# Attention's sums, maxima and quotients turned by VectorE's 32x32 block transposes in place of TensorE's transposes and the side PSUM bank

## The chip, the core and the metric

The kernel runs on one core of a Trainium2 chip. The metric is the device time of the launch in microseconds (us). One core has TensorE (PE, matrix products, with its weight loads PEld), VectorE (DVE), ScalarE (ACT), GpSimd (POOL) and SyncE (SP, which here only issues DMAs).

## What is computed

A transformer block over `x` of shape (4, 1024, 256): normalised attention with 16 heads of 16 dimensions, then a gated feed-forward network with ternary weights, each with a layer norm behind it and a residual.

```python
def _stable_softmax(x):
    x_max = jax.lax.stop_gradient(jnp.max(x, axis=-1, keepdims=True))
    exp_x = jnp.exp(jnp.clip(x - x_max, -50.0, 50.0))
    return exp_x / (jnp.sum(exp_x, axis=-1, keepdims=True) + EPS)
...
scores = jnp.einsum('bhqd,bhkd->bhqk', q, k) * scale
attn = _stable_softmax(scores)
out = jnp.einsum('bhqk,bhkd->bhqd', attn, v)
out = jnp.transpose(out, (0, 2, 1, 3)).reshape(B, S, D)
return out @ Wout.T
...
x = x + _layernorm(_L0_attn_ref(_layernorm(x, axis=-1), L0_attn_Wqkv, L0_attn_Wout), axis=-1)
x = x + _layernorm(_L0_ffn_ref(_layernorm(x, axis=-1), ...), axis=-1)
```

The kernel takes plain exponentials (no maximum is subtracted), so the reference's EPS has to be scaled by the largest exponential of a query: the quotient is `sum(e v) / (sum(e) + EPS * max(e))`. That is where sums, maxima and quotients come from.

## The kernel before

**Tiles and units.** Attention is cut into 32 units: batch `b` (4), group `g` of four heads (4), half `h` of the queries (2 of 512). In a unit every head has a slot of 32 partitions. A unit has 16 tiles; a tile is 128 keys by 512 queries for two heads. `exponentials(k)` (lines 521-529) makes a tile: two score matmuls `s` (L528) into one of three two-bank PSUM buffers (`ps`, tag `big`), and one ACT exponential `e` (L529) into a ring of eight. `weigh(k)` (L531-536) multiplies two tiles with the values: it accumulates into `acc`, one PSUM bank (`ps_acc`, one buffer), whose partition 32i+d is dimension d of head i, partition 32i+16 is the head's sum of exponentials, and whose 512 columns are queries. `rise(k)` (L538-545) keeps the running maximum over keys in `top` on DVE, for the first 128 queries of the half alone (the other queries need no EPS).

**The order.** A loop written out by hand (L1332-1363) makes three tiles, weighs what is ready, makes further tiles and then calls `side.take` once: a slot. `take` (L700-715) runs steps of the side chains that are due: at most one step with TensorE work in a slot (`Step(..., tensor=True)`), and steps without it as long as the slot's `room`, an estimate of DVE work, lasts. A step has a gap in slots, a flag for heavy ones (projections `p`, `pv`, `py`) and a `work` figure. The steps are: the next batch's layer norm and projections (`prologue`), the end of each unit (`divide`), the end of each half (`ending`), checks of the exponents' range (`bound`, `flag`), the loads of the stacks and the weights' rounding. All steps with a PSUM result share one bank, `misc` (L259-260).

**The end of a unit.** `unit_end` (L763-806) copies `acc` to SBUF as `o` (L328, DVE), which frees `acc`. `divide` (L558-584) sends `top` to DRAM and back as `folded`, which puts head and 32 keys on the partitions (L563, L566, SP queue); `fold` takes two maxima (L570); `run` puts four 128x128 TensorE transposes of `o` into the `misc` bank (L575) and a fifth of `folded` into unused columns of the same bank (`HOLE`, L577-578). Now queries are on the partitions: DVE reduces the maxima (`em`, L580), and `quotients` (L547-556) forms the denominators, inverts them and multiplies, into `on[h]` (128 queries x 4 x 256). The last group of the last batch uses `divide_last` (L586-600), which transposes `top` itself (L593) with no DRAM.

**The end of a half.** When its four groups are done, `ending` transposes `on` back in two steps of four TensorE transposes (L613) through `misc`, copies each to `oT` (L614; DVE, or ACT for the very last half), projects with the output weights `wo_sb` in two heavy steps `py` (L618-626), and then normalises and adds. For the last batch's second half these steps run among the first matmuls `pg` of the feed-forward network (`gated`, L924-940, one `side.take` after each pair of `pg` products, L1238-1241).

**The feed-forward network** (L924-1151) follows: matmuls `pg`, `ph` (L1015), `pz`, with two-term splits of the operands.

The lines that the change touches: the output weights' loads (L229-232), `on` (L249), `quotients`, `divide`, `divide_last`, `ending.transposes` (L606-616), the step list (L656) and `unit_end` (L766).

Of the kernel before, what the change touches and what calls it, by code (L numbers as in the profile page):

```python
# [10 lines left out]
F32 = mybir.dt.float32  # L11
# [4 lines left out]
ALU = mybir.AluOpType  # L16
AX = mybir.AxisListType
PSUM = bass.MemoryType.PSUM

P = 128  # L20
HEADS = 16
DH = 16
SLOT = 32
HPG = P // SLOT
# [1 line left out]
PARTS = 4  # L26
ROWS = PARTS * DH
RING = 8
HOLE = 20
TURN = 3  # L30
LN_EPS = 1e-5
SM_EPS = 1e-6
# [6 lines left out]
NQ = 512  # L39
WIDE = 1024  # L40
TPQ = NQ // P
# [89 lines left out]
def tile_fast(ctx: ExitStack, tc: tile.TileContext, x, wqk, wv, wo, w1, w1s, w2, w2s, h1, h1s, h2, h2s, w3, w3s, out, bad):  # L131
    nc = tc.nc
    B, S, D = x.shape
    HID = w1.shape[1]
    DC = D // P
    HC = HID // P
    NT = S // P
    NH = S // NQ
    HPT = P // DH
    GPT = HPT // HPG  # L140
# [3 lines left out]
    small = ctx.enter_context(tc.tile_pool(name="small", bufs=3))  # L144
# [52 lines left out]
    with ExitStack() as actx, ExitStack() as rctx:  # L197
# [21 lines left out]
        def load_rest():  # L219


            def load(out, in_):
                return lambda: nc.sync.dma_start(out=out, in_=in_)

            def load_half(b, h):
                return lambda: load_x(b, [h])

            rest = [load_half(2, h) for h in range(NH)]
            for c in range(DC):  # L229
                for h in range(HPT):  # L230
                    r = SLOT * (HPT * c + h)
                    rest.append(load(wo_sb[DH * h : DH * (h + 1), c, :], wo[r : r + DH, :]))
            rest += [load_half(b, h) for b in range(3, B) for h in range(NH)]
            rest += [load(scales[name], w) for name, w in (("w1", w1s), ("w2", w2s), ("h1", h1s), ("h2", h2s))]
            return rest + [load(w3s_sb, w3s.partition_broadcast(P))]
# [10 lines left out]
            nc.gpsimd.memset(t[:, :, :, DH : DH + 1], 1.0)  # L246
            vaug.append(t)

        on = [aw.tile([P, TPQ, D], F32, name=f"on{h}") for h in range(NH)]  # L249

        heads_bf = aw.tile([P, SLOT], BF16, name="heads_bf")
        nc.vector.memset(heads_bf, 0.0)
# [6 lines left out]
        def misc(name):  # L259
            return ps_misc.tile([P, NQ], F32, tag="misc", name=name)  # L260
# [66 lines left out]
        def to_vector(o, i, scale=1.0):  # L327
            nc.vector.tensor_scalar(o, i, scale, None, ALU.mult)  # L328
# [215 lines left out]
                top = tops[b, g, h]  # L544
                nc.vector.tensor_max(top, top if c > 1 else pair(k - 2)[:, :, :, 0:P], pair(k)[:, :, :, 0:P])  # L545

        def quotients(g, h, em, po):  # L547

            den = small.tile([P, TPQ, HPG], F32, tag="den", name="den")
            nc.vector.scalar_tensor_tensor(den[:, 0], em, SM_EPS, po[:, 0, :, DH], ALU.mult, ALU.add)  # L550
            nc.vector.tensor_copy(den[:, 1:], po[:, 1:, :, DH])
            nc.vector.reciprocal(den, den)
            nc.vector.tensor_mul(
                on[h][:, :, HPG * DH * g : HPG * DH * (g + 1)].rearrange("p t (i e) -> p t i e", e=DH),
                po[:, :, :, 0:DH], den.unsqueeze(3).to_broadcast([P, TPQ, HPG, DH]),
            )

        def divide(g, h, o, top):  # L558


            there = shuffle.tile([HPG, P, P], F32, tag="top", name="top_d")
            folded = work.tile([P, P // SLOT, P], F32, tag="folded", name="folded", bufs=1)
            nc.sync.dma_start(out=there.rearrange("i k q -> k i q"), in_=top.rearrange("p u n q -> p (u n) q"))  # L563

            def back():
                nc.sync.dma_start(out=folded, in_=there.rearrange("i (k s) q -> (i k) s q", s=P // SLOT))  # L566

            def fold():
                for n in (2, 1):
                    nc.vector.tensor_max(folded[:, 0:n], folded[:, 0:n], folded[:, n : 2 * n])  # L570

            def run():
                p = misc("po")
                for t in range(TPQ):
                    nc.tensor.transpose(p[:, t * P : (t + 1) * P], o[:, t * P : (t + 1) * P], ident)  # L575

                pm = p.rearrange("p (n s) -> p n s", s=SLOT)[:, :, HOLE : HOLE + P // (TPQ * HPG)]  # L577
                nc.tensor.matmul(pm, folded[:, 0], ident.rearrange("p (n k) -> p n k", n=TPQ * HPG), start=True, stop=True, is_transpose=True)
                em = small.tile([P, HPG], F32, tag="em", name="em")
                nc.vector.tensor_reduce(em, pm.rearrange("p (i n) k -> p i n k", i=HPG), AX.XY, ALU.max)  # L580
                po = p.rearrange("p (t i s) -> p t i s", t=TPQ, s=SLOT)
                quotients(g, h, em, po)

            return [Step(back, 2, False), Step(fold, 2, False, work=1), Step(run, 1, work=2)]

        def divide_last(g, h, o, top):  # L586


            def run():
                both = ps.tile([P, 2, NQ], F32, tag="big", name="po")  # L590
                po, pm = both[:, 0], both[:, 1].rearrange("p (i k) -> p i k", k=P)
                for i in range(HPG):
                    nc.tensor.transpose(pm[:, i], top[:, i // 2, i % 2], ident)  # L593
                for t in range(TPQ):
                    nc.tensor.transpose(po[:, t * P : (t + 1) * P], o[:, t * P : (t + 1) * P], ident)
                em = small.tile([P, HPG], F32, tag="em", name="em")
                nc.vector.tensor_reduce(em, pm, AX.X, ALU.max)
                quotients(g, h, em, po.rearrange("p (t i s) -> p t i s", t=TPQ, s=SLOT))

            return [Step(run, 1)]  # L600

        def ending(b, h, copy):

            st = {}

            def transposes(c):  # L606
                def run():
                    if c == 0:
                        st["oT"] = work.tile([P, DC, NQ], F32, tag="oT", name=f"oT_{b}_{h}", bufs=1)
                        st["y"] = (both if h else work).tile([P, TPQ, D], F32, tag="y", name=f"y_{b}_{h}", bufs=1)  # L610
                    pt = misc(f"po_{b}_{h}_{c}")
                    for t in range(TPQ):
                        nc.tensor.transpose(pt[:, t * P : (t + 1) * P], on[h][:, t, c * P : (c + 1) * P], ident)  # L613
                    copy(st["oT"][:, c, :], pt)  # L614

                return run

            def project(t0):  # L618
                def run():
                    py = misc(f"py_{b}_{h}_{t0}").rearrange("p (t d) -> p t d", d=D)  # L620
                    for i in range(2):
                        for c in range(DC):
                            by_slots(py[:, i, :], st["oT"][:, c, (t0 + i) * P : (t0 + i + 1) * P], wo_sb[:, c, :], start=c == 0, stop=c == DC - 1)
                    (copy if b == B - 1 else to_scalar)(st["y"][:, t0 : t0 + 2, :], py)

                return run

            def gather(i):
                def run():
                    st["mv"] = norms.gather([st["y"][:, j, :] for j in range(i, i + 2)], i, st.get("mv"))  # L630

                return run

            def root():
                st["ln"] = norms.root(st["mv"])

            def apply(i0):
                def run():
                    if b == B - 1 and i0 == 0:
                        st["to"] = norms.shift(st["ln"])  # L640
                    for i in range(i0, i0 + 2):
                        if b == B - 1:
                            norms.scale(st["y"][:, i, :], st["y"][:, i, :], st["to"], i)
                        else:
                            norms.apply(st["y"][:, i, :], st["y"][:, i, :], st["ln"], i)

                return run

            def residual(i):
                def run():  # L650
                    xr = xs[b][:, h * TPQ + i : h * TPQ + i + 2, :]
                    nc.vector.tensor_add(xr, xr, st["y"][:, i : i + 2, :])

                return run

            steps = [Step(transposes(c), 1, work=1) for c in range(DC)] + [Step(project(t), 2, heavy=True) for t in range(0, TPQ, 2)]  # L656
            tail = (
                [Step(gather(i), 1, False, work=1.6) for i in range(0, TPQ, 2)] + [Step(root, 0, False, work=0.3)]
                + [Step(apply(i), 1, False, work=1.2) for i in range(0, TPQ, 2)] + [Step(residual(i), 1, False, work=1) for i in range(0, TPQ, 2)]
            )  # L660
            if b < B - 1:

                return steps + [Step(lambda: side.add(tail), 0, False)]
            return steps + ([Step(open_ffn, 0, False)] if h == NH - 1 else []) + tail
# [98 lines left out]
        def unit_end(b, g, h):  # L763

            o = both.tile([P, NQ], F32, tag="o", name="o", bufs=2)
            to_vector(o, accs[b, g, h])  # L766
            unit = side.add((divide_last if (b, g) == (B - 1, NG - 1) else divide)(g, h, o, tops[b, g, h]), True)
            if b and not g:

# [837 lines left out]
```

## Time and profile before

| | |
|---|---|
| median of 3 runs | 1262.24 us (1261.6, 1262.24, 1263.4) |
| profiled execution | 1258.22 us, span 1256.4 us, mean TensorE clock 0.991 |
| attention stage (24 to 610 us), busy | PE 559.61, ACT 504.29, DVE 382.10, POOL 172.90 us |
| feed-forward stage (610 us to the end) | the rest of the span |
| `po<-ident,o` (L575), `po<-ident,folded` (L578), `po<-ident,on` (L613) | 120, 30 and 64 transposes |
| `po<-ident,top` (L593), `po<-ident,o` (L595) | 8 and 8 transposes |

The profiled execution took 1258.22 us from end to end; its span, from the first to the last instruction, is 1256.4 us. A row of the profile names line, engine, operation and tiles (written <- read), the count, the busy time and the mean of one. "Idle before" is how long the engine had nothing to do just before such an instruction, with what ended the wait. A matmul's duration contains its pipeline latency, so neighbouring matmuls overlap: their spacing is read from their start times. PEld is the load of the stationary operand.

### The profile page before, as it was taken

The numbers are of one execution on the slowest core, as the hardware profiler recorded it, in microseconds if no ns is written. First come the engines' busy times: TensorE is split into PE (matmuls) and PEld (weight loads), VectorE is DVE, ScalarE is ACT, GpSimd is POOL, SyncE is SP. The second block draws the span as 40 slices with busy tenths as digits, with TensorE's granted clock in tenths as the row PEclk, the third lists the DMA queues.
The fourth block names the chain that finished last, engine by engine and source line by source line (L and its number), as shares of the span: only waits on it lengthen the run. The fifth ranks groups of instructions, "written<-read, shape, count | busy, mean of one in ns | idle before, by whom it ended". The sixth has DMA issues, their size and how long they took to land.

```text
span 1256.4 us, 20888 instructions
## 1 busy us (share of the span) xinstructions
PE 1194.4 (95%) x7848; PEld 720.9 (57%) x7848; DVE 822.5 (65%) x1448; ACT 887.6 (71%) x1051; POOL 205.8 (16%) x279
## 2 busy tenths in 40 slices
PE   7999999999999999988999999999999999999994
PEld 3333334333333333323568788787888878888783
DVE  3567567776578656766666656767568675784756
ACT  4888788888888888998556564575756756566651
POOL 6211125452444332000000000000000000000000
PEclk9999999999999999999999999999999999999997
DMA  5776645765665665454204341254513545135401
GB/s 145 178 181 161 159 116 138 174 170 147 158 160 144 167 171 130 94 119 142 101 1 138 130 146 61 97 167 152 180 59 108 172 129 190 51 101 184 137 15 37
DMA packets 78670, 163.63 MB, mean 130 GB/s; under 512 B 14688, under 2 KB 40928, under 8 KB 78560
## 3 DMA queue, kind: packets, MB, share of 16 engines
q1 hardware_dynamic: 68624, 131.27, 37.9%
q0 software_dynamic: 9408, 30.42, 7.7%
q8 instruction: 64, 1.05, 0.4%
q10 hardware_dynamic: 528, 0.52, 0.1%
q14 instruction: 46, 0.38, 0.1%
HBM read 98.71 MB, written 29.88 MB: 102 GB/s over the span
## 4 chain that ended last, share of the span: by engine, by line
PE 65%; DVE 12%; ACT 12%; issue 5%; SPq 2%; DMA 2%; POOL 1%; ACTq 0%; POOLq 0%; DVEq 0%
PE ph L1015 25%; PE acc L536 13%; PE s L528 8%; PE pg L936 8%; ACT e L529 6%; PE p L322 4%; DVE lo L910 3%; ACT hi L906 2%; PE py L322 2%; SPq L476 2%; PE pv L322 2%; ACT w L1003 2%; DVE w L1026 2%; DVE u L1026 1%; DVE top L545 1%
## 5 line engine op out<-in xcount | busy, mean ns | idle before, releaser
L529 ACT ACTIVATE e<-s 128x1024 f32<-128x1024 f32 x512 | 482.4, 1034 | 56.9 <-PE s L528 46.9
L536 PE MATMUL acc<-e,vaug 128*32 128x512 f32 x2048 | 256.7, 604 | 2.7 <-POOL vaug L506 2.7
L528 PE MATMUL s<-sq,sk 64*128 64x512 f32 x1024 | 184.3, 441 | 17.5 <-ACT e L529 14.6
L1015 PE MATMUL ph<-hi,sq 128*128 128x512 f32 x448 | 178.3, 398 | 2.6 <-DVE u L1026 2.3
L1015 PE MATMUL ph<-hi,sk 128*128 128x512 f32 x448 | 176.7, 394 | 0.0
L1015 PE MATMUL ph<-lo,sq 128*128 128x512 f32 x448 | 176.6, 394 | 0.0
L1015 PE MATMUL ph<-lo,sk 128*128 128x512 f32 x448 | 176.4, 394 | 0.0
L108 POOL TENSOR_TENSOR rstd<-ve,minus_half 128x4 f32<-128x4 f32 (+1 forms) x34 | 38.0, 1118 | 767.2 <-DVE ve L106 708.2
L528 PEld LDWEIGHTS s<-sq,sk 64*128 64x128 f32 x1024 | 85.3, 184 | 136.6 <-ACT e L529 113.9
L545 DVE TENSOR_TENSOR top<-top,e 128x512 f32<-128x512 f32 x192 | 135.0, 703 | 11.9 <-ACT e L529 6.5
L536 PEld LDWEIGHTS acc<-e,vaug 128*32 128x32 f32 x2048 | 49.4, 109 | 108.2 <-issue 100.2
L910 DVE TENSOR_TENSOR lo<-c,hi 128x1024 fp32r<-128x1024 f32 x48 | 58.4, 1224 | 79.5 <-ACT hi L906 79.5
L1015 PEld LDWEIGHTS ph<-hi,sq 128*128 128x128 f32 x448 | 84.2, 188 | 24.0 <-DVE u L1026 4.0
L910 DVE TENSOR_TENSOR lo<-g,hi 128x1024 fp32r<-128x1024 f32 x48 | 58.8, 1225 | 58.0 <-ACT hi L906 57.7
L1015 PEld LDWEIGHTS ph<-hi,sk 128*128 128x128 f32 x448 | 84.1, 188 | 20.0
L1015 PEld LDWEIGHTS ph<-lo,sk 128*128 128x128 f32 x448 | 84.1, 188 | 19.9
L1015 PEld LDWEIGHTS ph<-lo,sq 128*128 128x128 f32 x448 | 84.2, 188 | 19.1
L1003 ACT ACTIVATE c<-ph,h_scale 128x512 f32<-128x512 f32 x64 | 40.6, 685 | 47.3 <-PE ph L1015 47.3
L938 ACT ACTIVATE sg<-pg,w_scale 128x512 f32<-128x512 f32 x64 | 43.5, 687 | 36.3 <-PE pg L936 33.6
L939 DVE SCALAR_TENSOR_TENSOR g<-pg,w_scale,sg 128x512 f32<-128x512 f32 x64 | 47.8, 747 | 30.1 <-ACT sg L938 30.0
L322 PE MATMUL p<-xT,wqk_sb 128*32 128x512 f32 x512 | 60.8, 593 | 5.6 <-ACT wqk_sb L210 2.6
L1119 PE MATMUL pz<-w_sb,lo 128*128 128x256 f32 x256 | 62.8, 287 | 3.2 <-DVE lo L910 3.2
(189 smaller groups left out, 1785.0 us busy)
## 6 DMA issues: line engine op xcount, KB each, us to landing
sq<-h_f SPq DMA_DIRECT2D x56, 512.0 KB, 3.8
sk<-h_f SPq DMA_DIRECT2D x56, 512.0 KB, 4.4
w<-in_h_dram POOLq DMA_DIRECT2D x32, 256.0 KB, 5.7
h_f<-wr POOLq DMA_DIRECT2D x16, 512.0 KB, 4.4
x<-in_h_dram SPq DMA_DIRECT2D x16, 512.0 KB, 3.5
top_d<-top SPq DMA_DIRECT2D x30, 256.0 KB, 2.3
folded<-top_d SPq DMA_DIRECT2D x30, 256.0 KB, 3.5
h_f<-wr POOLq DMA_DIRECT2D x16, 384.0 KB, 3.7
```

What stands on the lines that cost most here:

```text
L322: nc.tensor.matmul(o[j : j + SLOT, :], w[:, j : j + SLOT], i, **flags)
L528: nc.tensor.matmul(s[:, a, :], stacks[1, g % 2, u][r, c * P : (c + 1) * P], stacks[0, g % 2, u][r, h * NQ : (h + 1) * NQ], start=True, sto ...
L529: nc.scalar.activation(pair(k)[:, u], s, AF.Exp)
L536: nc.tensor.matmul(acc[SLOT * i : SLOT * (i + 1), :], vaug[g % 2][:, c, i, :], pair(k)[:, i // 2, i % 2, :], start=c == 0, stop=c == NT - 1)
L545: nc.vector.tensor_max(top, top if c > 1 else pair(k - 2)[:, :, :, 0:P], pair(k)[:, :, :, 0:P])
L910: nc.vector.tensor_sub(self.lo[i].t, self.raw[i].t, self.hi[i].t.bitcast(F32))
L936: nc.tensor.matmul(p[:, k, :], homes[n][d][:, m * P : (m + 1) * P], half[:, d, :], start=d == j == 0, stop=d == DC - 1 and j == 1)
L938: nc.scalar.activation(sg, p[:, 0, :], AF.Silu, scale=scales["w1"][:, m : m + 1])
L939: nc.vector.scalar_tensor_tensor(x[i, h][c // 2].t[:, c % 2, :], p[:, 1, :], scales["w2"][:, m : m + 1], sg, ALU.mult, ALU.mult)
L1003: nc.scalar.activation(o.t[:, j, :], (o.t if src is None else src)[:, j, :], AF.Gelu, scale=scale[:, m : m + 1])
L1015: nc.tensor.matmul(p[:, j, :], w, half, start=start and c == n == 0, stop=c == HC // 2 - 1 and n == 1, skip_group_check=True,)
L1119: nc.tensor.matmul(p[:, j, :D], half[:, (t0 + j) * P : (t0 + j + 1) * P], homes["w3"][c], start=c == order[0] and n == 0, stop=c == order[ ...
```

## The change

The attention core's results are turned by `nc.vector.transpose`, which transposes every 32x32 block of a tile by itself, on DVE. A block transpose of `acc` (partitions head i, slot s; columns block j, query q of 32) gives `o` with partition 32i+q and column 32j+s: queries lie on the partitions within each head's 32, and the slots on the columns. So `unit_end`'s copy becomes a block transpose, `fold` ends with a 128x128 block transpose of `folded`, `em` and `quotients` read SBUF with no PSUM bank, and `on[h]` is laid out as 2 x 16 blocks x 32. `ending` turns `on` back with one block transpose of 128x512 per half of the columns, straight into `oT`. The rows of `oT` then stand in another order (head in group, group, dimension), and the output weights' rows are loaded in that order. The steps `run` of `divide` and `transposes` of `ending` no longer count as tensor steps; they carry `work` 1.4 and 0.7, and `fold` 1.2. `divide_last` turns `top` by a block transpose of 128x512, reduces, gathers the four partition groups with four small copies, reduces, and spreads the result with four small copies.

```diff
-                    r = SLOT * (HPT * c + h)
+                    r = SLOT * (HPT * c + HPG * (h % GPT) + h // GPT)
                     rest.append(load(wo_sb[DH * h : DH * (h + 1), c, :], wo[r : r + DH, :]))
...
-        on = [aw.tile([P, TPQ, D], F32, name=f"on{h}") for h in range(NH)]
+        on = [aw.tile([P, DC, NQ // SLOT, SLOT], F32, name=f"on{h}") for h in range(NH)]
...
-        def quotients(g, h, em, po):
-
-            den = small.tile([P, TPQ, HPG], F32, tag="den", name="den")
-            nc.vector.scalar_tensor_tensor(den[:, 0], em, SM_EPS, po[:, 0, :, DH], ALU.mult, ALU.add)
-            nc.vector.tensor_copy(den[:, 1:], po[:, 1:, :, DH])
+        def quotients(g, h, em, o):
+
+            o = o.rearrange("p (j s) -> p j s", s=SLOT)
+            den = small.tile([P, NQ // SLOT], F32, tag="den", name="den")
+            n = P // SLOT
+            nc.vector.scalar_tensor_tensor(den[:, 0:n], em, SM_EPS, o[:, 0:n, DH], ALU.mult, ALU.add)
+            nc.vector.tensor_copy(den[:, n:], o[:, n:, DH])
             nc.vector.reciprocal(den, den)
-            nc.vector.tensor_mul(
-                on[h][:, :, HPG * DH * g : HPG * DH * (g + 1)].rearrange("p t (i e) -> p t i e", e=DH),
-                po[:, :, :, 0:DH], den.unsqueeze(3).to_broadcast([P, TPQ, HPG, DH]),
-            )
+            e = DH * (g % GPT)
+            nc.vector.tensor_mul(on[h][:, g // GPT, :, e : e + DH], o[:, :, 0:DH], den.unsqueeze(2).to_broadcast([P, NQ // SLOT, DH]))
...
             def fold():
                 for n in (2, 1):
                     nc.vector.tensor_max(folded[:, 0:n], folded[:, 0:n], folded[:, n : 2 * n])
+                nc.vector.transpose(folded[:, 1], folded[:, 0])
 
             def run():
-                p = misc("po")
-                for t in range(TPQ):
-                    nc.tensor.transpose(p[:, t * P : (t + 1) * P], o[:, t * P : (t + 1) * P], ident)
-
-                pm = p.rearrange("p (n s) -> p n s", s=SLOT)[:, :, HOLE : HOLE + P // (TPQ * HPG)]
-                nc.tensor.matmul(pm, folded[:, 0], ident.rearrange("p (n k) -> p n k", n=TPQ * HPG), start=True, stop=True, is_transpose=True)
-                em = small.tile([P, HPG], F32, tag="em", name="em")
-                nc.vector.tensor_reduce(em, pm.rearrange("p (i n) k -> p i n k", i=HPG), AX.XY, ALU.max)
-                po = p.rearrange("p (t i s) -> p t i s", t=TPQ, s=SLOT)
-                quotients(g, h, em, po)
-
-            return [Step(back, 2, False), Step(fold, 2, False, work=1), Step(run, 1, work=2)]
+                em = small.tile([P, P // SLOT], F32, tag="em", name="em")
+                nc.vector.tensor_reduce(em, folded[:, 1].rearrange("p (j k) -> p j k", k=SLOT), AX.X, ALU.max)
+                quotients(g, h, em, o)
+
+            return [Step(back, 2, False), Step(fold, 2, False, work=1.2), Step(run, 1, False, work=1.4)]
...
             def run():
-                both = ps.tile([P, 2, NQ], F32, tag="big", name="po")
-                po, pm = both[:, 0], both[:, 1].rearrange("p (i k) -> p i k", k=P)
+                turned = work.tile([P, P // SLOT, P], F32, tag="folded", name="turned", bufs=1)
+                flat, n = top.rearrange("p u n q -> p (u n q)"), HPG * P // SLOT
+                nc.vector.transpose(turned.rearrange("p s q -> p (s q)"), flat)
+                nc.vector.tensor_reduce(flat[:, 0:n], turned.rearrange("p s (j k) -> p (s j) k", k=SLOT), AX.X, ALU.max)
+                parts = flat[0:SLOT, n : n + n * P // SLOT].rearrange("p (k n) -> p k n", n=n)
+                for k in range(P // SLOT):
+                    nc.vector.tensor_copy(parts[:, k], flat[SLOT * k : SLOT * (k + 1), 0:n])
+                most = flat[0:SLOT, P : P + n]
+                nc.vector.tensor_reduce(most, parts.rearrange("p k n -> p n k"), AX.X, ALU.max)
+                most = most.rearrange("p (i j) -> p i j", i=HPG)
+                em = small.tile([P, P // SLOT], F32, tag="em", name="em")
                 for i in range(HPG):
-                    nc.tensor.transpose(pm[:, i], top[:, i // 2, i % 2], ident)
-                for t in range(TPQ):
-                    nc.tensor.transpose(po[:, t * P : (t + 1) * P], o[:, t * P : (t + 1) * P], ident)
-                em = small.tile([P, HPG], F32, tag="em", name="em")
-                nc.vector.tensor_reduce(em, pm, AX.X, ALU.max)
-                quotients(g, h, em, po.rearrange("p (t i s) -> p t i s", t=TPQ, s=SLOT))
-
-            return [Step(run, 1)]
+                    nc.vector.tensor_copy(em[SLOT * i : SLOT * (i + 1), :], most[:, i])
+                quotients(g, h, em, o)
+
+            return [Step(run, 1, False)]
...
-                    pt = misc(f"po_{b}_{h}_{c}")
-                    for t in range(TPQ):
-                        nc.tensor.transpose(pt[:, t * P : (t + 1) * P], on[h][:, t, c * P : (c + 1) * P], ident)
-                    copy(st["oT"][:, c, :], pt)
+                    nc.vector.transpose(st["oT"][:, c, :], on[h][:, c].rearrange("p j s -> p (j s)"))
...
-            steps = [Step(transposes(c), 1, work=1) for c in range(DC)] + [Step(project(t), 2, heavy=True) for t in range(0, TPQ, 2)]
+            steps = [Step(transposes(c), 1, False, work=0.7) for c in range(DC)] + [Step(project(t), 2, heavy=True) for t in range(0, TPQ, 2)]
...
-            to_vector(o, accs[b, g, h])
+            nc.vector.transpose(o, accs[b, g, h])
```

More of the change, by code (lines that the diff above doesn't have):

```diff
@@ L28 @@
 RING = 8
-HOLE = 20
 TURN = 3
```

## The prediction

> **What bounds the kernel now.** I read the page's busy shares first, then the busy time of the attention stage, then the timeline of TensorE and ScalarE around the end of a unit, then the waits, then the groups by form.
>
> ```profile
> PE 1194.4 (95%) x7848; PEld 720.9 (57%) x7848; DVE 822.5 (65%) x1448; ACT 887.6 (71%) x1051; POOL 205.8 (16%) x279
> 24.00:610.00 586.00, 559.61 (x4746) 210.75 (x4746) 382.10 (x832) 504.29 (x554) 172.90 (x229) 1.00 0.59 148
> ```
>
> The second line is the attention stage (length, then busy PE, PEld, DVE, ACT, POOL, the clock, DMA). 559.61 of 586 us looks like a full TensorE, but it holds pipeline latency. By start times a tile takes about 0.30 us of `s` and 0.43 us of `acc`, against 0.94 us of `e` on ScalarE (482.4 us over 512). So for a tile alone ScalarE is the slower; what side steps put between two batches of `s` decides whether it starves. ScalarE is idle 586 - 504.3 = 82 us in the stage. The timeline of PE and ACT at one unit's end shows how:
>
> ```profile
> 586.29 1.92 PE L536 MATMUL acc<-e,vaug 128*32 128x512 f32 x16
> 588.14 0.66 PE L575 MATMUL po<-ident,o 128*128 128x128 f32 x4
> 588.64 0.27 PE L578 MATMUL po<-ident,folded 128*128 128x128 f32 x1
> 588.84 0.96 PE L528 MATMUL s<-sq,sk 64*128 64x512 f32 x6
> ...
> 583.88 4.69 ACT L529 ACTIVATE e<-s 128x1024 f32<-128x1024 f32 x5
> 589.44 5.61 ACT L529 ACTIVATE e<-s 128x1024 f32<-128x1024 f32 x6 [0.88 <-PE s L528]
> ```
>
> The five transposes hold TensorE from 588.14 to 588.84, 0.70 us; the next `s` starts only then, and its first exponential at 589.44, 0.88 us after ScalarE had run out. Three score buffers hold at most 2.8 us of exponentials, less than `acc` (1.85), transposes (0.70) and the latency of `s` (0.60) together.
>
> ```profile
> DVE em L580 <- PE po L578: 28.0, 21, 2.4
> ACT e L529 <- PE s L528: 46.9, 63, 2.7
> DVE oT L328 <- PE po L613: 12.2, 8, 2.3
> ```
>
> VectorE too stands idle for TensorE's turns, 28.0 + 12.2 us (us in total, times, longest). Prices:
>
> ```profile
> L575 PE MATMUL po<-ident,o 128*128 128x128 f32 x120 | 19.7, 287 | 2.9 <-DVE norm L420 2.9
> L613 PE MATMUL po<-ident,on 128*128 128x128 f32 x64 | 10.4, 285 | 0.0
> L328 DVE TENSOR_SCALAR o<-acc 128x512 f32<-128x512 f32 x32 | 22.1, 690 | 16.4 <-PE acc L536 15.8
> L580 DVE TENSOR_REDUCE em<-po 128x4 f32<-128x128 f32 x30 | 8.7, 290 | 28.2 <-PE po L578 28.0
> L570 DVE TENSOR_TENSOR folded<-folded 128x128 f32<-128x128 f32 x30 | 8.8, 294 | 1.0
> ```
>
> [...] they follow each other at 0.14 us, so five cost 0.70 us. [...] No row of this trace shows a block transpose[...].
>
> **The unknown price.** The trace's 128x128 and 128x512 fp32 operations take 294 and 690 ns, 1.03 ns for a further element. [...] I take 0.71 us for 128x512 and 0.31 for 128x128[...]. Lower end 0.49 us, the trace's cheapest 128x512 operation (a memset, 485 ns); upper end twice the price, 1.4 us[...].
>
> **Part by part.**
>
> *TensorE loses 230 transposes.* In the stage: 30 blocks of five at 0.70 us = 21.0; 14 blocks of four (`on`, 56 transposes) at 0.58 = 8.1; one end of `divide_last` at 1.47 (593.78 to 595.25). Together 30.6 us; 2.1 us more lie in the feed-forward stage (8 + 8 transposes). What of it is on the path: I went through all blocks in the timeline and took the smaller of the block and ScalarE's next idle stretch behind it. 28 of 30 `po` blocks are followed by 0.50 to 1.41 us of idle: 17.5 us. 7 of the 14 `on` blocks are: 3.9 us. The end of `divide_last`: 0.8. Together 22.2 us. A second count: cut at the starts of the `s` batches, a slot of three tiles takes 3.70 us with a `po` block (31 of them, `divide_last` counted), 3.16 with an `on` block (14), and 2.76 with nothing (35). Replaced by empty slots they would give 31 x 0.94 + 14 x 0.40 = 34.7 us; but 2.76 is below ScalarE's own 3 x 0.94 = 2.82 and lives on the idle of dense slots before it, and `po` slots hold more `acc` work. At 2.82 and with 0.13 us taken off for that it is 31 x 0.75 + 14 x 0.34 = 28. I take 24: the 22.2 and about a quarter of the 8.4 us whose blocks had no idle behind them, as TensorE's lead is given back at a later heavy step.
>
> *The steps become free of TensorE.* At most one tensor step runs in a slot, so 45 slots open and the projections move up into them. The heavy steps are the same in number (about 3.8 to 4.1 us a slot each); in the built order they still stand mostly apart, 79 of some 170 slots being empty where 35 were. The DMAs are the same, in slightly another order (27 differing rows on SP, 24 on POOL); the stack loads they carry have slack (one wait of 1.3 us on them at `s`): nothing. The output weights' rows: the same 16 loads per column half, nothing.
>
> *VectorE.* `o`: 32 x (0.71 - 0.69) = 0.6; `oT`: 16 x 0.71 for 14 x 0.69, 1.7; the new turn of `folded`: 30 x 0.31 = 9.3. `em` and the quotients have the same sizes, now from SBUF: nothing. Together about +12 us, while 40 us of standing idle go. It is busy 382 of 586 us: hidden by that, and at a real cost only through `acc`, which has one buffer. The copy of `o` ends 0.05 to 2.74 us before the next `acc` (median 1.05). At +0.02 us this is nothing; at twice the price (+0.7) the slacks below it sum to about 4 us lost. The new turn adds no wait on another engine: what follows it on VectorE (`top`, `lo`) is later by 0.31 us and earlier by about 0.9 for the wait on `po` that is gone.
>
> *The last two units.* VectorE gets per unit a turn of 0.71, a reduction of 0.69, eight small copies at 0.16 (as the 128x12 copy), a small reduction near 0.29, for one reduction of 0.69: +2.3 us. In the second this stands ahead of a product `g`, on which the third `pg` buffer waits (0.41 us of wait there now): about 2 us lost, against 2.1 us of transposes taken out and the two `oT` copies (0.59 each) off ScalarE. Sum nothing, between -2 and +2.
>
> **The sum.** Against the profiled execution: 1258.2 - 24 = 1234 us. That execution lies 4.0 us below the median of 1262.24, so the forecast is 1262.2 - 24 = 1238 us.
>
> **Rivals.**
>
> *ScalarE takes the place.* Taken over whole units (16 tiles: ScalarE 15.0 us plus its copies, TensorE 11.6 plus its steps), the sum of the larger of both falls only from 527 to 515 us, 12 us; the rest becomes TensorE waiting for `e`. For it: 113.9 us of PEld waiting for `e` already. Against: the idle stretches behind 28 of 30 blocks, those of late, light units too. 1250 us.
>
> *All of it comes off*, and VectorE's 40 us of idle help the maxima and the projections too: the second count, 28 to 33. 1230 us.
>
> *VectorE becomes the bound.* [...] each unit's `acc` is freed later, and TensorE waits at its next `acc`. By the measured slacks the loss is 19 us at +1.6 us, 24 at +1.8, 39 at +2.3: it eats the gain once a 128x512 turn costs about 2.5 us. At 3 us: 1262 - 24 + 39 = 1277. [...]
>
> *The change doesn't do what it says*: excluded, since the built program holds 230 fewer transposes.
>
> **Chances.** Forecast 0.53 (its own range 1234 to 1244); ScalarE 0.21 (1244 to 1255, price up to double included); all of it 0.17 (1226 to 1234); VectorE 0.05; within 0.2% by mishaps that I can't name 0.04. The range 1229 to 1250 leaves out about 2 in 10. Faster by over 0.2% (2.5 us, about what a measurement of this kernel can tell from no change) 0.91, same 0.04, slower 0.05.
>
> **What would show it.** Right: `o<-acc` near 0.71 us and `folded` near 0.31; the stage ends near 586 us instead of 610; ScalarE's idle falls from 82 to about 58 us; the waits on `po` are gone; the feed-forward stage is unchanged. Wrong: PEld's wait for `e` grows by some 12 us more than ScalarE's idle shrinks (the first rival); waits of `acc` for `o`, now 1.5 us, grow to tens (VectorE); a gap of over 2 us after the first `pg` (the last unit).

## The result and the profile after

| | before | after |
|---|---|---|
| median of the runs | 1261.92 us (4 runs) | 1247.05 us (4 runs, 1245.36 to 1248.18) |
| ratio, 95% interval | | 0.9886 [0.9864, 0.9907] |
| profiled execution | 1258.22 us, span 1256.4 | 1248.18 us, span 1246.4 |

The change makes the kernel 14.9 us faster. 1238 us was forecast, a gain of 24; 1247.05 lies inside the range of 1229 to 1250 and near its upper end. The changed kernel was measured twice more beside other kernels: 1243.22 us, ratio 0.9851 [0.9833, 0.9869], and 1244.08 us, ratio 0.9867 [0.9839, 0.9895], against 1262.47 and 1260.18 us. So the gain is 15 to 19 us by three comparisons, all short of 24. By the prediction's own division (1234 to 1244 for the forecast, 1244 to 1255 for the rival that ScalarE takes the place) 1247.05 falls to the rival, 1243.22 to the forecast and 1244.08 on the border.

First the page's busy shares, then the stage that answers to the one shown of before (length, busy PE, PEld, DVE, ACT, POOL, clock, DMA), here to 600 us:

```profile
PE 1178.4 (95%) x7618; PEld 700.5 (56%) x7618; DVE 843.7 (68%) x1500; ACT 884.3 (71%) x1049; POOL 204.0 (16%) x279
```

```profile
24.00:600.00 576.00, 544.86 (x4580) 192.26 (x4576) 402.93 (x876) 503.40 (x556) 174.28 (x233) 0.99 0.61 152
```

TensorE has 230 instructions fewer (7848 to 7618) and VectorE 52 more. ScalarE's work in the stage is what it was (504.3 and 503.4 us); its idle time went from 82 to 73.

At a unit's end, where the five transposes stood, the timeline of PE and ACT now shows this:

```profile
575.07 1.92 PE L535 MATMUL acc<-e,vaug 128*32 128x512 f32 x16
576.93 0.97 PE L527 MATMUL s<-sq,sk 64*128 64x512 f32 x6
577.83 1.07 PE L535 MATMUL acc<-e,vaug 128*32 128x512 f32 x8
...
571.74 5.61 ACT L528 ACTIVATE e<-s 128x1024 f32<-128x1024 f32 x6 [0.82 <-DVE top L544]
577.53 4.69 ACT L528 ACTIVATE e<-s 128x1024 f32<-128x1024 f32 x5 [0.18 <-PE s L527]
```

The next `s` follows `acc` at once, and ScalarE's wait for it is 0.18 us where it was 0.88: the 0.70 us of the block came off one for one. The waits (us in total, times, longest) tell what that became in sum, the first line before the change and the others after it:

```profile
PEld s L528 <- ACT e L529: 113.9, 191, 2.0
PEld s L527 <- ACT e L528: 168.7, 267, 2.5
ACT e L528 <- PE s L527: 24.9, 41, 2.3
ACT e L528 <- DVE top L544: 11.5, 11, 2.9
```

ScalarE's wait for scores is down from 46.9 to 24.9 us. These 22 us equal the direct count of the prediction (22.2), but they are not what ScalarE won: from the first `e` to the first `pg` all its waits together fell from 81.0 to 68.0 us, 13 us. Its wait for the maxima `top` rose from 4.1 to 11.5 us, that for the projections' products `p`, which it copies, from 18.6 to 21.7, and that for `py` from 5.4 to 8.5. And TensorE's wait for `e` grew from 113.9 to 168.7 us. The waits of VectorE on `po`, 28.0 and 12.2 us, are gone. The chain of waits, 25 to 600 us, says the same of before and of after:

```profile
by line: PE acc L536 26.6%; PE s L528 17.4%; ACT e L529 13.8%; PE p L322 7.3%; issue 4.9%; SPq L476 4.1%; PE pv L322 3.9%; PE py L322 3.3%; DVE top L545 2.9%; PE po L575 2.4%; DMA wo_sb<-in_wo_dram 1.0%; DVE st L98 0.9%; PE po L613 0.7%; DM
```

```profile
by line: PE acc L535 22.8%; ACT e L528 20.0%; PE s L527 14.9%; PE p L321 7.7%; issue 6.0%; DVE top L544 4.7%; PE pv L321 3.6%; PE py L321 3.2%; SPq L475 2.8%; DMA sk<-ck0lo 1.2%; DVE folded L569 1.0%; DMA sk<-ck1hi 0.9%; DMA sq<-cq0lo 0.7%;
```

The two `po` entries (3.1%) have left the chain, and the exponentials have gone from 13.8 to 20.0% of it.

**Where the time went.** The profiled execution of the first table isn't the best one to compare: TensorE's granted clock fell to half (0.50) for 3.4 us twice in its opening, for 6.8 us in its last unit and once more behind the first `pg` (last section), which the profiled execution of before did not have. The second profiled execution of the changed kernel (`after_again`, span 1239.5 us) has half-clock spells where before has them. Between those two the span fell by 16.9 us. I cut both at the first exponential of a unit and set beside it the prediction's direct count, summed over the blocks of the same stretch (us):

| stretch | counted | before | after_again | difference |
|---|---|---|---|---|
| opening, to the first `e` | 0 | 25.0 | 25.5 | +0.5 |
| batch 0 (units 0 to 7) | 4.0 | 151.9 | 152.1 | +0.2 |
| batch 1 | 6.7 | 147.3 | 142.8 | -4.5 |
| batch 2 | 5.2 | 146.9 | 140.7 | -6.2 |
| batch 3 but its last unit | 4.3 | 119.3 | 114.5 | -4.8 |
| last unit, to the first `pg` | 1.9 | 20.5 | 20.0 | -0.5 |
| the rest | 0 | 645.6 | 644.0 | -1.6 |
| sum | 22.1 | 1256.4 | 1239.5 | -16.9 |

Batches 1 to 3 give 15.5 of the 16.2 us counted there (15.1 and 12.8 in the two other profiled executions of the changed kernel, the latter with two more half-clock spells there, and a granted clock of 0.988 over the whole execution where `after_again` has 0.992). What is missing is batch 0, which gave nothing (-0.5 and -0.6 us in the other two), and the last unit.

In batch 0 ScalarE did wait less for scores, 11.8 us where it was 17.6. But it waited as much more for `p`, 12.7 where it was 6.4 (12.8 and 12.3 in the other two). Two places make most of it; before, then `after_again`, timeline of ACT:

```profile
88.84 0.60 ACT L325 ACTIVATE cq0hi<-p 128x512 fp32r<-128x512 f32 x1 [0.45 <-PE p L322]
143.53 2.85 ACT L529 ACTIVATE e<-s 128x1024 f32<-128x1024 f32 x3 [2.74 <-PE s L528]
```

```profile
84.49 0.60 ACT L324 ACTIVATE cq0hi<-p 128x512 fp32r<-128x512 f32 x1 [2.08 <-PE p L321]
146.16 0.60 ACT L324 ACTIVATE ck1hi<-p 128x512 fp32r<-128x512 f32 x1 [3.42 <-PE p L321]
```

The first is a product `p` that VectorE's `norm` held up (shown in the section on why). The second stands behind a wait of TensorE for a stack load in unit 6, and behind the half-clock spell that follows it; before, a like stall at that load goes by the name of scores.

### The profile page after: what moved, and what is told of

Same layout as the page of the kernel before. It is cut to its first block, busy times and chain, and to the rows that moved or that the text cites. A ratio compares the mean times of both kernels' runs of the same rounds, so it can differ in the third digit from the quotient of the medians.

```text
span 1246.4 us, 20490 instructions
## 1 busy us (share of the span) xinstructions
PE 1178.4 (95%) x7618; PEld 700.5 (56%) x7618; DVE 843.7 (68%) x1500; ACT 884.3 (71%) x1049; POOL 204.0 (16%) x279
## 4 chain that ended last, share of the span: by engine, by line
PE 60%; ACT 15%; DVE 15%; issue 5%; DMA 2%; SPq 2%; ACTq 0%; POOL 0%; POOLq 0%; DVEq 0%
PE ph L1010 25%; PE acc L535 11%; ACT e L528 9%; PE pg L931 8%; PE s L527 7%; PE p L321 4%; DVE lo L905 3%; ACT hi L901 2%; DVE top L544 2%; PE py L321 2%; ACT w L998 2%; PE pv L321 2%; DVE w L1021 2%; DVE u L1021 1%; SPq L475 1%
## 5 line engine op out<-in xcount | busy, mean ns | idle before, releaser
L528 ACT ACTIVATE e<-s 128x1024 f32<-128x1024 f32 x512 | 480.9, 1039 | 37.7 <-PE s L527 24.9
L527 PE MATMUL s<-sq,sk 64*128 64x512 f32 x1024 | 194.1, 450 | 24.3 <-ACT e L528 20.2
L527 PEld LDWEIGHTS s<-sq,sk 64*128 64x128 f32 x1024 | 87.4, 185 | 185.9 <-ACT e L528 168.7
L544 DVE TENSOR_TENSOR top<-top,e 128x512 f32<-128x512 f32 x192 | 138.3, 720 | 21.1 <-ACT e L528 16.5
L321 PE MATMUL p<-xT,wqk_sb 128*32 128x512 f32 x512 | 64.9, 628 | 6.1 <-ACT wqk_sb L209 2.6
```

Source lines behind the costliest of these rows:

```text
L321: nc.tensor.matmul(o[j : j + SLOT, :], w[:, j : j + SLOT], i, **flags)
L527: nc.tensor.matmul(s[:, a, :], stacks[1, g % 2, u][r, c * P : (c + 1) * P], stacks[0, g % 2, u][r, h * NQ : (h + 1) * NQ], start=True, sto ...
L528: nc.scalar.activation(pair(k)[:, u], s, AF.Exp)
```

## The experiments

All are edits of the changed kernel except one, `x11_before_few_max`. The theory of the prediction (TensorE's blocks fed ScalarE late) stands against the rivals: ScalarE takes the place, VectorE takes the place, or the steps' new order does it.

**The steps marked as before.** The block transposes stay, but their steps have the old kernel's marks and prices:

```diff
-            return [Step(back, 2, False), Step(fold, 2, False, work=1.2), Step(run, 1, False, work=1.4)]
+            return [Step(back, 2, False), Step(fold, 2, False, work=1), Step(run, 1, work=2)]
...
-            steps = [Step(transposes(c), 1, False, work=0.7) for c in range(DC)] + ...
+            steps = [Step(transposes(c), 1, work=1) for c in range(DC)] + ...
```

(and `Step(run, 1)` in `divide_last`.)

> The changed kernel, but the turning steps keep their tensor flag, gap and work figure as before: TensorE has the kernel before's order with the transposes simply missing, and no step moves up into the opened slots. If the forecast's direct count holds (each block removed gives the idle behind it, 22 us) and the shortfall comes from packing the projections into the opened slots, it takes about 1240 us, below the changed kernel's 1247. If ScalarE is the bound whatever the order, or VectorE is late whatever the order, it takes 1245 to 1250.

1249.79 us, 0.9896 [0.9868, 0.9924], beside before alone. The interval overlaps those of the changed kernel (0.9886, 0.9851 and 0.9867), and the median lies 3 to 7 us above theirs: the new marks cost nothing overall that these runs can tell, and what they gain, if anything, isn't resolved. The timeline of TensorE shows where this one lost what it had gained in batch 0:

```profile
135.18 0.61 PE L527 MATMUL s<-sq,sk 64*128 64x512 f32 x2
141.09 1.49 PE L527 MATMUL s<-sq,sk 64*128 64x512 f32 x3 [5.31 <-DMA sq<-cq1lo]
```

Its units 0 to 5 took 109.1 us where before took 111.3, and then `s` stood 5.31 us for a stack load (1.28 us in before); batch 0 came to 152.0 us all the same: it arrived earlier at this load and waited longer for it. The changed kernel doesn't arrive earlier; its units 0 to 5 take 111.7 to 111.9 us in its three profiled executions. So in these executions batch 0 loses its gain at the load with the old marks, and ahead of it with the new ones.

**TensorE's work put back.** As `e1_flags`, and TensorE makes the transposes besides, into the `misc` bank, with nobody reading them:

```diff
             def run():
+                p = misc("po")
+                for t in range(TPQ):
+                    nc.tensor.transpose(p[:, t * P : (t + 1) * P], o[:, t * P : (t + 1) * P], ident)
+                nc.tensor.transpose(p[:, 0:P], folded[:, 0], ident)
...
+                    pt = misc(f"po_{b}_{h}_{c}")
+                    flat = on[h][:, c].rearrange("p j s -> p (j s)")
+                    for t in range(TPQ):
+                        nc.tensor.transpose(pt[:, t * P : (t + 1) * P], flat[:, t * P : (t + 1) * P], ident)
```

> As e1, with TensorE transposes put back into the same steps (five per unit into the misc bank, four per half column in the ending), their results unused: VectorE's block transposes stay. Not put back are the 16 transposes of the last two units. If TensorE's time was all that the change saved, it returns to 1258 to 1262 us; if VectorE's shorter waits are worth something by themselves, it stays below that, near 1255; if the block transposes cost VectorE more than they save, it lies above 1262.

1262.22 us, 1.0007 [0.9994, 1.0021]: the time of before. Its waits, 25 to 600 us:

```profile
PEld s L527 <- ACT e L528: 115.9, 196, 2.0
ACT e L528 <- PE s L527: 43.4, 60, 2.7
```

Both are back where before had them (113.9 and 44.8 in this window), with all of VectorE's new work in place and nobody waiting for the transposes' results. So the gain is TensorE's time, and it is 12.4 us against `e1_flags`, for some 30 us of transposes. With the transposes comes back their use of the one `misc` bank, which this run doesn't part from them; but TensorE stands idle only 2.5 us ahead of them for another use of that bank (2.9 before), so by these waits the bank is a small part.

**The maxima of the last unit but one.** For that half alone, `divide_last` leaves the maxima out:

```diff
+                if h == 0:
+                    nc.vector.memset(em, 1.0)
+                else:
```

> The changed kernel, but the maxima of the last group's first half are left out (em is set to 1, which only enters times 1e-6): its turn, two reductions and eight small copies on VectorE are gone. If the burst of VectorE work at the end of the last unit but one, behind which the running maximum was 2.9 us late for the ring, and the half-clock spell after it, cost what the trace suggests, it takes about 4 us less than the changed kernel, 1243. If ScalarE is the bound anyway it gains under 1 us.

1239.61 us, 0.9824 [0.9799, 0.9849], 4 to 7 us below the three medians of the changed kernel, none of which was measured beside it; the last unit takes 17.2 us instead of 20.0 to 22.7 in the three executions of the changed kernel. The timeline of `after_again` shows the burst, and who waits behind it:

```profile
579.77 0.67 DVE L585 STREAM_TRANSPOSE turned<-top 128x512 f32<-128x512 f32 x1
580.48 0.69 DVE L586 TENSOR_REDUCE top<-turned 128x16 f32<-128x512 f32 x1
581.20 0.69 DVE L589 COPY top<-top 32x16 f32<-32x16 f32 x4
582.21 0.68 DVE L595 COPY em<-top 32x4 f32<-32x4 f32 x4
...
585.16 0.68 DVE L544 TENSOR_TENSOR top<-e,e 128x512 f32<-128x512 f32 x1
585.94 7.44 ACT L528 ACTIVATE e<-s 128x1024 f32<-128x1024 f32 x8 [2.90 <-DVE top L544]
587.02 0.51 PE L527 MATMUL s<-sq,sk 64*128 64x512 f32 x2 [1.57 <-ACT e L528]
```

From 579.77 VectorE works off the burst, the quotients and two copies; the next unit's first maximum comes at 585.16, and the exponential that overwrites a buffer which this maximum reads waits 2.90 us for it. TensorE waits behind that.

**The same maxima on TensorE.** `divide_last` with 16 small products in place of the burst:

```diff
+                pm = ps.tile([P, 2, NQ], F32, tag="big", name="pm")[:, 0].rearrange("p (j k) -> p j k", k=P)
+                for j in range(P // SLOT):
+                    for i in range(HPG):
+                        nc.tensor.matmul(pm[SLOT * i : SLOT * (i + 1), j], top[:, i // 2, i % 2, SLOT * j : SLOT * (j + 1)], ident, start=True, stop=True)
...
+                nc.vector.tensor_reduce(em, pm, AX.X, ALU.max)
```

> The changed kernel, but in the last group the running maxima are turned by TensorE (16 products of 32 columns by 128 with the identity into a score buffer) and reduced once by VectorE, in place of the block transpose, two reductions and eight small copies; complete, with the sums still turned by VectorE. If the burst on VectorE costs what leaving out the maxima showed (5 to 7 us), it takes 1241 to 1243 us. If that gain was chance of the opening, 1247.

1241.06 us, 0.9848 [0.9827, 0.9869], beside 1243.22 for the changed kernel. Taken again:

> The changed kernel with the last group's maxima turned by TensorE, a second time beside the changed kernel on one chip: if the burst is worth what the trace shows (2.7 us up to the first product of the feed-forward network, 2 us given back behind it), it stands 1 to 4 us below the changed kernel.

1243.79 us, 0.9869 [0.9847, 0.9891], beside 1244.08. No gain that can be told. In the profiled executions the last unit is shorter (18.2 and 18.3 us against 20.0 and 21.0), but from the first `pg` to the end they are longer (646.1 and 647.0 us against 644.0 and 643.6). There they hold one and two half-clock spells more, some 1.5 us each (last section; the granted clock over the whole execution is 0.990 and 0.986 against 0.992 and 0.988), so whether the edit itself gives time back behind `pg` isn't shown.

**The turn of `folded` left out.** `em` reduces the unturned maxima:

```diff
-                nc.vector.transpose(folded[:, 1], folded[:, 0])
...
-                nc.vector.tensor_reduce(em, folded[:, 1].rearrange("p (j k) -> p j k", k=SLOT), AX.X, ALU.max)
+                nc.vector.tensor_reduce(em, folded[:, 0].rearrange("p (j k) -> p j k", k=SLOT), AX.X, ALU.max)
```

> The changed kernel, but the block transpose of folded is left out (em is reduced from the unturned tile, so the maxima that enter times 1e-6 are of other queries): 30 x 0.31 = 9.3 us less on VectorE. If VectorE's lateness holds back the rest of the gain, it takes 2 to 4 us less than the changed kernel, about 1244. If VectorE has room, no difference, 1247.

1243.65 us, 0.9861 [0.9834, 0.9888], within the three results of the changed kernel. Of the 30 x 0.31 us of VectorE most is hidden, as forecast; a gain of 2 to 4 us can't be told from none here.

**A turn twice as dear.** The block transpose of `acc` issued twice:

```diff
             nc.vector.transpose(o, accs[b, g, h])
+            nc.vector.transpose(o, accs[b, g, h])
```

> The changed kernel, with the turn of each unit's sums from PSUM to SBUF issued twice: 32 x 0.72 = 23 us more on VectorE, and the accumulation bank freed 0.72 us later per unit. By the slacks of the copy in the kernel before (median 1.05 us) alone it costs about 4 us: 1251. If VectorE is what holds back the changed kernel, much of the 23 us shows: 1260 or more. If only ScalarE and the score buffers bind, 1248.

1254.72 us, 0.9942 [0.9926, 0.9957], 11.5 us over the changed kernel measured beside it; its runs spread from 1247.88 to 1255.77. The waits of TensorE for the second turn, 52 to 600 us:

```profile
PE acc L535 <- DVE o L762: 7.4, 13, 0.9
```

In the changed kernel `acc` waits 1.7 us for `o`. The 5.7 us more are near the 4 that the slacks gave, and the stretch from the first `o` to the first `pg` is 4.6 us longer than in `after_again`. This profiled execution was the fastest of its runs, with a mean TensorE clock of 0.991 where the six others have 0.984 to 0.987. So the other half of the 11.5 us isn't in it; half-clock spells are a likely place, but no trace of a slower execution shows it.

**Work taken off ScalarE.** The projected result `y` is copied by VectorE in all batches, 12 copies of 0.60 us off ScalarE:

```diff
-                    (copy if b == B - 1 else to_scalar)(st["y"][:, t0 : t0 + 2, :], py)
+                    copy(st["y"][:, t0 : t0 + 2, :], py)
```

> The changed kernel, with the projected output copied out of PSUM by VectorE instead of ScalarE in all batches: 12 x 0.60 us less on ScalarE, 12 x 0.69 us more on VectorE in the attention stage. If ScalarE is the bound there, it takes 4 to 7 us less, 1241. If VectorE is as late as ScalarE, no difference or slower by 2 to 4 us.

1250.18 us, 0.9899 [0.9879, 0.9919], 7 us over the changed kernel measured beside it. From the first `o` to the first `pg` ScalarE works 476.1 us instead of 480.9, and its waits sum to 74.5 instead of 59.7. Its wait for scores, 52 to 600 us:

```profile
ACT e L528 <- PE s L527: 40.4, 51, 4.5
```

Relief of ScalarE did not show through. But the run is not a clean one: VectorE got the copies instead, TensorE's products `y` wait for it, and the profiled execution holds five half-clock spells in that stretch where `after_again` has one (granted clock 0.98 there, against 1.00), so part of the 40.4 us is theirs. It shows that ScalarE's own work isn't what alone sets the time; it doesn't tell a gain of a few us there from a loss on VectorE.

**The changed kernel again**, beside the last three:

> The changed kernel itself once more, beside the others on the same chip: 1247 us within 3 us; by how much its opening differs from that of the first profiled execution (first turn of sums at 55.7 us, against 52.1 before) tells what of the difference between profiled executions is the opening's clock and not the change.

1243.22 us, as given above.

**Most maxima left out, after and before.** Six of a unit's seven maxima are dropped, which frees VectorE:

```diff
-            if c:
+            if c == 1:
```

> The changed kernel with six of the seven running maxima of each unit left out (only the first two key tiles enter the maximum, which enters times 1e-6): 192 x 0.70 = 134 us less on VectorE in the attention stage. If VectorE's lateness took back the rest of the expected gain, it takes 8 to 12 us less than the changed kernel, about 1233. If ScalarE with its three score buffers is what binds, the maxima lie beside it and only the burst's 3 to 5 us go: 1239.

1234.80 us, 0.9802 [0.9779, 0.9825], 9.3 us under the changed kernel measured beside it. The same edit of the kernel before:

> The kernel before with the same six of seven running maxima left out. It tells whether VectorE's lateness was a cost already: if it is new with the change, this stays within 2 us of the kernel before, 1261; if it was there before too, it falls by as much as the changed kernel does, to about 1250.

1253.24 us, 0.9939 [0.9917, 0.9961], 6.9 us under before. So the maxima on VectorE cost 7 us before the change and 9 after it; with nearly none of them the change is worth 1253.2 - 1234.8 = 18.4 us, with them 16.1 beside it. The 2.3 us between these lie within the noise (each of the ratios is uncertain by some 3 us), so VectorE explains at most a few us of the missing gain. Most of what both kernels win, 6 us each, they win in batch 0: it takes 145.1 us in `x10_few_max` and 145.8 in `x11_before_few_max`, instead of 151.3 to 152.1. In neither of the two does TensorE wait for the stack load of batch 0 any more. So batch 0 is held in both kernels by VectorE's maxima and by what waits behind them; but even with VectorE relieved the change gains only 0.7 us there, and the cause of that was not found.

**The changed kernel a third time**, beside these:

> The changed kernel once more, as the reference for x10 and x7_again on the same chip: 1243 to 1247 us.

1244.08 us.

**A wait that looks like VectorE and isn't.** Ten of the eleven waits of ScalarE for `top` are 0.5 to 1.3 us, seven of them 0.82. `after_again`, timeline of ACT and DVE:

```profile
309.91 2.85 ACT L528 ACTIVATE e<-s 128x1024 f32<-128x1024 f32 x3
313.58 1.94 ACT L528 ACTIVATE e<-s 128x1024 f32<-128x1024 f32 x2 [0.82 <-DVE top L544]
...
312.80 0.69 DVE L544 TENSOR_TENSOR top<-e,e 128x512 f32<-128x512 f32 x1 [2.06 <-ACT e L528]
```

and the same place in `x10_few_max`, where VectorE has little to do:

```profile
308.87 1.94 ACT L528 ACTIVATE e<-s 128x1024 f32<-128x1024 f32 x2 [0.82 <-DVE top L544]
...
308.09 0.69 DVE L544 TENSOR_TENSOR top<-e,e 128x512 f32<-128x512 f32 x1 [2.31 <-ACT e L528]
```

VectorE had itself waited for ScalarE. Nine of the eleven stand at such a place: in every third unit the hand-written order issues the first maximum after the exponential of tile 8, which refills half of the buffer that this maximum reads; tile 9's exponential refills the other half and must let the maximum pass: 0.69 us and the two hand-overs, 0.13 us together. By start times the 11 exponentials of tile 9 in these units come 22.2 us in sum after those of tile 8 before the change, and 22.5 after it. They are no part of what changed. In before the profile puts five of these gaps down to `top` and the others to other releasers, so the growth of that row from 4.1 to 11.5 us is a change of name, but for the 2.90 us of the burst. An order without these gaps was not tried.

## Why the prediction was right, and by how much it was off

The range held, but it held the first rival's 1250 as well, and the measured 1247.05 lies nearer to that than to 1238. Of the signs named in advance the waits on `po`, the prices of the turns and the feed-forward stage came; ScalarE's idle fell to 73 us instead of 58, and the stage ended at 601 us (595.5 and 599.0 in the other two executions) instead of 586.

*TensorE loses 230 transposes* ("I take 24"): right in mechanism, too high in size. `e2_pe_added` shows that the gain is TensorE's time. In batches 1 to 3 the direct count came out, 15.5 us for 16.2 counted. The term fails in two places. In batch 0 it counted 4.0 us, and nothing came: the idle stretch behind a block was taken for lost time, but ScalarE, served earlier there, waited for the next late thing instead, the products `p` and what stands behind the stack load. And the quarter of the uncovered blocks (1.8 us), expected from a lead that is handed on, did not show: TensorE's surplus became waiting for `e` (+55 us). That the three score buffers cap its lead is the likely reason; no run had another number of buffers. The second count, by slots, was further off: slots with no side work did replace those with a block, 79 where 35 were, but the slots of the projections rose, for instance `p` from 4.10 to 4.25 us and `py` from 3.84 to 4.19.

*The steps become free of TensorE* ("nothing"): not contradicted in sum, since `e1_flags` is not clearly slower or faster than the changed kernel; but in batch 0 the marks did matter (units 0 to 5 take 109.1 us with the old ones, in one profiled execution, and 111.7 to 111.9 with the new, in three). The sentence that the stack loads "have slack" failed for batch 0: one wait of 1.3 us is no slack. Counted from the first exponential, that wait ends at 112.5 us before, at 113.3 to 114.0 in the changed kernel and at 113.7 in `e1_flags`, so the load is nearly a fixed date. With the projections moved up one more wait arose in `after_again`:

```profile
82.50 1.92 PE L321 MATMUL p<-xT,wqk_sb 128*32 128x512 f32 x16 [1.47 <-DVE norm L419]
```

*The price of a block transpose* (0.71 and 0.31 us): right. The changed kernel's rows by tile (min, median, max in ns):

```profile
L761 DVE STREAM_TRANSPOSE o<-acc x32: 701/717/718, 55.7 to 601.3; 128x512 f32<-128x512 f32 x32
L570 DVE STREAM_TRANSPOSE folded<-folded x30: 310/311/315, 65.4 to 574.3; 128x128 f32<-128x128 f32 x30
L609 DVE STREAM_TRANSPOSE oT<-on x16: 667/702/714, 183.7 to 612.4; 128x512 f32<-128x512 f32 x16
```

The prediction took both prices with no row of before that shows a block transpose; measured there was only the 1.03 ns for a further element. In fp32 a turn of 128x128 takes 311 ns here, and one of 128x512 takes 717 ns from PSUM (`acc`) and 702 from SBUF (`on`). The 406 ns between 311 and 717 for 384 further elements per partition are 1.06 ns each, near the 1.03 ns of the plain operations that the prediction used. The doubled price that it allowed for, 1.4 us for 128x512, didn't come.

*VectorE, +12 us, hidden*: busy time between the first `o` and the first `pg` grew by 19 us (372.2 to 391.2 us). The turns of `folded` are 9.3 of it, as forecast; the burst of the last unit but one, 3 us, lies in that stretch and was not in the 12; and operations of unchanged size lasted a little longer, the 217 maxima by 3.9 us together and the small ones of the denominators by 2.0. How much of it shows is not resolved: at most a few us by the two kernels with few maxima and by `e4_no_max_turn`, and the burst.

*The last two units* ("sum nothing"): half wrong. I priced the burst only in the last unit, where it is ahead of `g`, and there it cost nothing to be seen: the rest after the first `pg` is 1.6 us shorter. In the unit before, I left it out, with the counted gain of 1.9 us standing; it has 2.90 us of ScalarE waiting behind it, and the gain there came to 0.5.

*The rivals.* ScalarE takes the place: the result lies between its 12 us and the forecast's 24, and its sign is there, with PEld's wait for `e` up 55 us while ScalarE's idle shrank by some 14: 41 us more, where the prediction asked for 12. How much of the shortfall is its mechanism, ScalarE's own work as the bound, stays open: `x9_y_vector` took the copies off ScalarE and lost time, but VectorE had to take them. All of it comes off: out by the runs. VectorE becomes the bound: out at this price; with the turn doubled the kernel still is faster than before, 0.9942 [0.9926, 0.9957].

The sum as it was found, against `after_again`: 24 forecast, less 4.2 in batch 0, 2.2 in batch 1, 1.4 in the last unit, 1.9 that was added to the count, 0.5 in the opening, plus 1.0 in batch 2, 0.5 in batch 3, 1.6 after the first `pg`: 16.9. The first two minuses have a cause that the traces show only in part; a single execution of each kernel stands behind each entry.

## What to carry to other kernels

Idle time of the fed engine right behind a step that is removed is a sound count of the gain only as far as the next date that doesn't move: look along the trace for a wait on a load or on another engine's late work, and count what lies ahead of it as nothing. A wait that shrinks by the amount that was counted proves little until the engine's other waits are added up. A burst of small operations is to be priced at every place where it stands, by who is queued behind it on its engine, however small its sum. And a row of waits says who came last, not who was late: where the releaser itself had waited for the waiting engine, it is the order of the instructions that costs.

## What the runs showed of the hardware

TensorE's granted clock falls to half (0.50) in spells of 3.41 us, at different places in different executions. In the traces of the first table they begin at 139.1 and 797.9 us before the change and at 14.5, 21.3, 144.2, 591.3 (two in a row), 635.7 and 789.3 us after it; one more, from 1241.6 and from 1233.0 us, lasts to the end. Two executions of the changed kernel in the last unit, first the one at 1248.18 us (its timeline, and a window with length, busy times, and the clock in the third column from the end), then `after_again`:

```profile
592.43 1.93 PE L535 MATMUL acc<-e,vaug 128*32 128x512 f32 x8
```

```profile
591.00:594.50 3.50, 3.08 (x14) 0.69 (x14) 1.65 (x4) 3.40 (x4) 0.00 (x0) 0.54 0.00 0
```

```profile
589.28 1.06 PE L535 MATMUL acc<-e,vaug 128*32 128x512 f32 x8
```

The same eight products take 1.93 instead of 1.06 us. In the two traces of the first table all spells begin a whole number of 3.4133 us apart, to within 0.002 us, over up to 357 such steps. In the 3.41 us ahead of each of the six that begin later than 30 us from the start and earlier than 20 us before the end, TensorE is idle for 1.44 to 2.17 us by the profile; 1.84 us of idle, from 782.5 us on after the change, went without a spell right behind it. So idle time alone doesn't tell where a spell comes, and the same stall (2.90 us of ScalarE, here) brings one in one execution and none in the next; what decides it was not shown. The opening shows the price: with no spell in it the first exponential starts at 25.0 to 26.0 us (six executions of six kernels or repeats), with one at 26.4 to 27.4 (three), with two at 28.3 to 28.9 (five). That is some 1.5 us for a spell. In the two traces, before has a granted clock of 1.00 from 0 to 27 us and its first exponential at 25.0 us, after has 0.87 and 28.7 us: in its two spells 16 products `p` take 3.48 us instead of 1.92 and 32 take 5.34 instead of 3.64, 3.3 us together. This is one reason why medians of one kernel differ by 4 us, and why a single profiled execution is not enough to size a gain of 15.
